# Score tiles from three equally wide matmuls over placed query copies, in a cross-attention kernel

## The chip, the cores and the metric

The kernel runs on one core of a Trainium2 chip. The metric is the device time in microseconds (us). Five engines work side by side: TensorE (PE in the profile, its weight loads PEld), VectorE (DVE), ScalarE (ACT), GpSimd (POOL) and SyncE (SP, which here issues most DMA transfers).

## The reference, cut to what matters

Per batch `b` of 32, 512 positions with 640 channels attend to 77 context positions with 1024 channels, in 20 heads of 32 channels:

```python
q = _heads(hidden_states @ to_q_w)
h_txt = _sdpa(q, _heads(ehs_txt @ to_k_w), _heads(ehs_txt @ to_v_w))
out = _merge(h_txt) @ to_out_w + to_out_b
out = out + residual          # residual = hidden_states
```

`_sdpa` is softmax(q k^T / sqrt(32)) v. The other three context parts of the reference are empty here, since the context has 77 rows, all of them text. All is float32.

## The kernel before, in words

**Parts.** Float32 products are made of two rounded parts: each operand is split into a high part (a rounded copy) and a low part (what the rounding left). A product is the sum of three matmuls: high x high, high x low, low x high. So every query or key needs its high and its low part in SBUF.

**Stages.** A fill computes keys and values of all batches on TensorE, splits them and stores them in DRAM (`k_dram`: 128 channels x high and low x channel chunk x all key rows). Attention then goes batch by batch. A batch has five units, n = 5 b + j, one for each chunk j of 128 channels, that is four heads. For each unit:

- `queries` (L536, token q0 to q4): 15 matmuls of 512 columns into the one `pq` bank of PSUM.
- `high_query` (L777, token Q, ScalarE) writes the high part, `copy_query` (L781, tokens k0, k1, GpSimd) copies halves of it, `low_query` (L785, tokens g0, g1, VectorE) subtracts and writes low parts. Together they fill `qt`, three stationary tiles of 128 rows.
- `score_tile` (L563, tokens s0 to s3, one for each 128 of the 512 positions): three matmuls into one of three `sc` banks: 308 columns (high tile against all four heads' high keys) and twice 154 columns (for two heads each, a tile that holds high queries in one half of its rows and low queries in the other).
- `score_max` (m, VectorE), `exps` (e, ScalarE, one instruction per head with the sum of its row), `sums` (r), `normalize` (N, GpSimd), `block_transpose` (z, VectorE, into the one `z` buffer), and `store_p` (w, four DMA transfers of the probabilities to DRAM).
- Four units later: `load_rows` (d, DMA back, transposed), splitting (c, R on VectorE, l on GpSimd), six value matmuls (v), adding of two halves (A, a), splitting of the result (h, L), and the output projection of a whole batch (p, 120 matmuls of 320 columns), with bias and residual (b, f) and the store (o).
- x of the following batch is loaded (ux), transposed (T) and split (X on ScalarE, x on GpSimd).

**Keys.** The units of a batch form two groups, chunks 0 to 2 and chunks 3 and 4. Each group has one key buffer, `kb0` and `kb1`, of four planes. `load_head_keys` (L514, tokens uk) brings, by one DMA each, one head's high or low keys of the whole group to the rows of its place: eight transfers per group and batch. `copy_half_keys` (L517, token K, GpSimd) then copies 64 rows of two of the planes into planes 0 and 3, so that the wide matmul has only the high keys with zeros around them. All other places stay zero from a memset. The key buffers are single: a group's keys for the next batch are loaded after the last score of the group in this batch.

**What sets the order.** The order of all instructions is written out by hand as three lists of tokens: FILL (batches 0 and 1 among the last products of keys and values), PLAN (the loop, run for batches 2 to 30, 29 times) and LAST_ (batch 31 and the ends). A token names the unit (a digit j, with 5 for the next batch's unit 0) and the step; a query token `jq`, `jQ`, `jk`, `jg` works for the unit after j. Each engine executes its own instructions in the order of the list, and SyncE its transfers. L886 `issue` and L963 `special` translate tokens to calls.

The three matmuls of a score tile before, where `half` is 154 and the keys' planes are the first index of `kb`:

```python
(slice(0, KCOLS), kb[:, 0::3, jg]),
(slice(0, half), kb[:, 1, jg]),
(slice(half, KCOLS), kb[:, 2, jg]),
```

Of the kernel before, what the change touches and what calls it, by code (L numbers as in the profile page):

```python
# [23 lines left out]
P = 128  # L24
Q = 32
# [6 lines left out]
NBLK = HPC * KPAD // Q  # L32

# [18 lines left out]
def kernel(  # L52
# [394 lines left out]
    def open_small():  # L447
        nonlocal small
        if small is None:
            kvc.release()  # L450
            xpool.append(ctx.enter_context(tc.tile_pool(name="xparts", bufs=1, reuse_waits="tile")))
            small = ctx.enter_context(tc.tile_pool(name="small", bufs=1, reuse_waits="tile"))
            kbs.append(small.tile([P, 4, GROUPS[0][1], KCOLS // 2], FPR, name="kb0"))
# [9 lines left out]
    def open_second():  # L463
        nonlocal z
        if not vbs:
# [3 lines left out]
            kbs.append(pool.tile([P, 4, GROUPS[1][1], KCOLS // 2], FPR, name="kb1"))  # L469
# [33 lines left out]
    def load_keys(b, g, heads=range(HPC), parts=(0, 1)):  # L503
        j0, nj = GROUPS[g]
        src = k_dram[g][:, :, :, b * NKEY : (b + 1) * NKEY].bitcast(F32)
        kb = kbs[g].bitcast(F32)
        for i in heads:
            own, half = slice(i * HD, (i + 1) * HD), slice(i % 2 * NKEY, (i % 2 + 1) * NKEY)
            other = slice(*((i + 2) % HPC * HD + k for k in (0, HD)))
            for part, rows in enumerate((own, other)):  # L510
                if part in parts:
                    nc.sync.dma_start(kb[rows, 1 + i // 2, :, half], src[own, part])

    def load_head_keys(b, g, i, part):  # L514
        load_keys(b, g, (i,), (part,))

    def copy_half_keys(g, h):  # L517
        kb, rows = kbs[g], slice(64 * h, 64 * h + 64)
        nc.gpsimd.tensor_copy(kb[rows, 3 * h], kb[rows, 1 + h].bitcast(F32))

    def copy_keys(g):
        copy_half_keys(g, 0)
        copy_half_keys(g, 1)
# [26 lines left out]
    def split_q(n):  # L550

        qt, pq = qts[n % 2], pqs.pop(n)
        nc.scalar.copy(qt[:, 0, :], pq)
        lower, upper = slice(0, 64), slice(64, P)
        halves = ((lower, upper), (upper, lower))
        for w, (r, other) in enumerate(halves):
            nc.gpsimd.tensor_copy(qt[other, 1 + w, :], qt[r, 0, :].bitcast(F32))
        for w, (r, other) in enumerate(halves):
            nc.vector.tensor_tensor(
                qt[r, 1 + w, :], pq[r], qt[r, 0, :].bitcast(F32), ALU.subtract  # L560
            )

    def score_tile(n, t):  # L563
        b, j = divmod(n, NC_)
        g = GROUP_OF[j]
        qt, kb = qts[n % 2], kbs[g]
        jg = j - GROUPS[g][0]
        sc = ps.tile([P, S], F32, tag="sc", name="sc", bufs=3)
        half = KCOLS // 2
        for m, (cols, keys_) in enumerate(  # L570
            (
                (slice(0, KCOLS), kb[:, 0::3, jg]),
                (slice(0, half), kb[:, 1, jg]),
                (slice(half, KCOLS), kb[:, 2, jg]),
            )
        ):
            nc.tensor.matmul(  # L577
                sc[:, cols],
                qt[:, m, t * P : (t + 1) * P],
                keys_,  # L580
                start=(m == 0),
                stop=(m == 2),
            )
        return sc

    def score_max(sc):
        nm = small.tile([P, HPC], F32, tag="nm", name="nm", bufs=3)
        nc.vector.tensor_reduce(  # L588
            nm, sc[:, :KCOLS].rearrange("p (h k) -> p h k", k=NKEY), AX.X, ALU.max, negate=True
        )  # L590
        return nm

    def scores(n, t):
        sc = score_tile(n, t)
        return sc, score_max(sc)

    def exps(n, t, sc, nm):
        if n not in sms:
            sms[n] = small.tile([P, NQ * HPC], F32, tag="sm", name="sm", bufs=2)
        for i in range(HPC):  # L600
            at = t * HPC + i
            nc.scalar.activation(  # L602
                pnb[n % 2][:, at, :NKEY],
                sc[:, i * NKEY : (i + 1) * NKEY],
# [172 lines left out]
    def high_query(n):  # L777
        open_first()
        nc.scalar.copy(qts[n % 2][:, 0, :], pqs[n])  # L779

    def copy_query(n, w):  # L781
        qt, half = qts[n % 2], (slice(0, 64), slice(64, P))
# [345 lines left out]
```

## Time and profile before

| | |
|---|---|
| median of three runs | 1859.1 us (1857.3 to 1859.61) |
| the profiled execution's span | 1856.5 us |
| TensorE busy | 1842.4 us, 10332 matmuls |
| VectorE, ScalarE, GpSimd busy | 1563.4, 1527.2, 1303.9 us |
| TensorE's clock granted | 1.00 |
| DMA | 431.37 MB in 563296 packets |

The span runs from the first instruction's start to the last one's end, and lies 2.6 us under the median of the timed runs. A row of the groups gives the line, engine and operation, the tiles it writes and reads, the shape, the count, the busy time and the mean of one instruction in ns, and after the last bar the idle time of the engine just before, with what ended it. Matmuls are pipelined, so the printed length of one is longer than its distance to the next one; the distance of two starts is what it costs.

### The profile page before, as it was taken

To read this page: it belongs to the slowest core of one execution; us is meant where nothing else is said; L and a number is where in the kernel's file an instruction comes from. 1 tells how busy PE (TensorE), PEld (TensorE's weight loads), DVE (VectorE), ACT (ScalarE), POOL (GpSimd) and SP (SyncE) were. 2 spreads that over 40 slices of the span, in tenths; PEclk is the share of its full clock that TensorE was granted. 3 is DMA by queue.
4 is the path that set the end of the run, shared out by engine and by line. 5 is a ranking of instruction groups with operands and counts; after the bars stand their busy time and mean duration, and the time that the engine had idled before them with its cause. 6 is when DMAs were issued, how large, how long until landed. Compare 5 with 4: busy or idle time off the path is not lost.

```text
span 1856.5 us, 37492 instructions
## 1 busy us (share of the span) xinstructions
PE 1842.4 (99%) x10332; PEld 1655.7 (89%) x10332; DVE 1563.4 (84%) x2502; ACT 1527.2 (82%) x6218; POOL 1303.9 (70%) x1120
## 2 busy tenths in 40 slices
PE   9999999999999999999999999999999999999998
PEld 7888897889999999999999999999999999999998
DVE  5445458899999999999999999999999999999996
ACT  3233248899999999999999999999999999999984
POOL 1100268778788788778778877887778878877874
PEclk9999999999999999999999999999999999999999
DMA  9889779998998898888998888998889988888875
GB/s 188 199 198 249 184 193 256 254 242 235 247 240 243 240 238 232 242 235 236 238 244 237 234 243 237 244 238 237 235 234 244 244 241 236 237 232 243 228 228 187
DMA packets 563296, 431.37 MB, mean 232 GB/s; under 512 B 191120, under 2 KB 471120, under 8 KB 563088
## 3 DMA queue, kind: packets, MB, share of 16 engines
q1 hardware_dynamic: 558192, 413.16, 84.5%
q0 software_dynamic: 4800, 15.65, 2.7%
q8 instruction: 85, 1.39, 0.3%
q14 instruction: 123, 1.01, 0.2%
q10 hardware_dynamic: 96, 0.16, 0.0%
HBM read 247.17 MB, written 181.64 MB: 231 GB/s over the span
## 4 chain that ended last, share of the span: by engine, by line
PE 93%; DMA 4%; SPq 1%; DVE 1%; ACT 1%; issue 0%; POOL 0%; DVEq 0%; ACTq 0%; POOLq 0%
PE po L750 29%; PE pq L542 28%; PE pa L694 12%; PE sc L577 11%; PE pv L204 7%; PE pk L204 6%; DMA pd<-z 1%; DMA cs<-in_ctx_dram 1%; DMA xr<-in_x_dram 1%; DMA wo_s<-wo_dram 0%; DMA wraw<-in_L_xattn_to_v_w_dram 0%; DMA xs<-in_x_dram 0%; DMA wraw<-in_L_xattn_to_k_w_dram 0%; ACT pn L602 0%; DMA raw<-pd 0%
## 5 line engine op out<-in xcount | busy, mean ns | idle before, releaser
L602 ACT ACTIVATE pn<-sc,nm 128x77 f32<-128x77 f32 x2560 | 797.1, 343 | 36.0 <-DVE nm L588 29.6
L750 PE MATMUL po<-wo_s,at 128*128 128x320 f32 x3840 | 707.2, 310 | 0.1
L750 PEld LDWEIGHTS po<-wo_s,at 128*128 128x128 f32 x3840 | 619.7, 188 | 41.1 <-DVE xr L765 0.6
L542 PE MATMUL pq<-xt,wq_s 128*128 128x512 f32 x2400 | 596.7, 394 | 2.9 <-ACT pp L661 1.9
L602 ACT ACTIVATION_READ_ACCUMULATOR pn<-sc,nm 128x1 f32 x2560 | 567.5, 222 | 0.0
L542 PEld LDWEIGHTS pq<-xt,wq_s 128*128 128x128 f32 x2400 | 436.7, 188 | 82.5 <-ACT pp L661 2.1
L617 POOL TENSOR_TENSOR pn<-pn,rs 128x1232 f32<-128x1232 f32 x160 | 389.4, 2434 | 94.0 <-DVE rs L612 90.0
L694 PE MATMUL pa<-pp,vb 128*128 128x512 f32 x960 | 340.9, 403 | 4.1 <-DVE at L731 3.3
L577 PEld LDWEIGHTS sc<-kb,qt 128*128 128x128 f32 x1920 | 302.9, 188 | 14.4 <-ACT pn L602 1.8
L588 DVE TENSOR_REDUCE nm<-sc 128x4 f32<-128x308 f32 x640 | 295.0, 466 | 21.6 <-PE sc L577 16.7
L577 PE MATMUL sc<-kb,qt 128*128 128x154 f32 (+1 forms) x1920 | 301.9, 274 | 0.9 <-ACT pn L602 0.9
L783 POOL CAST qt<-qt 64x512 fp32r<-64x512 f32 x320 | 196.9, 615 | 139.5 <-ACT qt L779 124.4
L712 DVE TENSOR_TENSOR pa<-pa,aw 64x512 f32<-64x512 f32 x320 | 222.3, 695 | 50.4 <-ACT aw L708 43.2
L679 POOL TENSOR_TENSOR pp<-raw,pp 64x512 fp32r<-64x512 f32 x160 | 207.0, 1294 | 66.9 <-ACT pp L661 53.5
L624 DVE STREAM_TRANSPOSE z<-pn 128x1280 f32<-128x1280 f32 x160 | 241.2, 1507 | 8.8 <-DMA pd<-z 3.4
L708 ACT COPY aw<-pa 64x1024 f32<-64x1024 f32 x160 | 162.2, 1014 | 85.0 <-PE pa L694 83.9
L787 DVE TENSOR_TENSOR qt<-pq,qt 64x512 fp32r<-64x512 f32 x320 | 216.8, 678 | 13.9 <-ACT qt L779 9.0
L320 POOL TENSOR_TENSOR xt<-xs,xt 128x512 fp32r<-128x512 f32 x160 | 204.6, 1305 | 20.8 <-ACT xt L316 15.8
L743 POOL TENSOR_TENSOR xr<-xr,bias 128x640 f32<-128x640 f32 x128 | 202.3, 1581 | 13.1 <-issue 3.5
L672 DVE TENSOR_TENSOR pp<-raw,pp 128x1024 fp32r<-128x1024 f32 x160 | 195.7, 1223 | 0.0
L694 PEld LDWEIGHTS pa<-pp,vb 128*128 128x128 f32 x960 | 173.8, 189 | 15.1 <-DVE pp L672 2.3
L663 ACT CAST pp<-raw 128x1024 fp32r<-128x1024 f32 x160 | 168.1, 1051 | 0.7 <-DMA raw<-pd 0.7
(46 smaller groups left out, 1584.2 us busy)
## 6 DMA issues: line engine op xcount, KB each, us to landing
pd<-z SPq DMA_DIRECT2D x640, 160.0 KB, 3.4
raw<-pd SPq DMA_DIRECT2D x160, 512.0 KB, 4.5
xr<-in_x_dram SPq DMA_DIRECT2D x128, 320.0 KB, 3.9
out_dram<-xr SPq DMA_DIRECT2D x127, 320.0 KB, 3.7
xs<-in_x_dram SPq DMA_DIRECT2D x124, 320.0 KB, 5.8
raw<-pd SPq DMA_DIRECT2D x160, 128.0 KB, 4.2
v_dram<-vs SPq DMA_DIRECT2D x80, 192.0 KB, 4.0
k_dram<-ks POOLq DMA_DIRECT2D x20, 512.0 KB, 4.2
```

Source lines behind the costliest of these rows:

```text
L204: nc.tensor.matmul(held[j][:, :gn], w[:, k, a, :], cts[g, k][:, c, :gn], start=(k == 0 and n == 0), stop=(k == NK - 1 and n == 2),)
L542: nc.tensor.matmul(pqs[n], wq_s[:, k, a, j * P : (j + 1) * P], xts[b, k][:, c, :], start=(k == 0 and m == 0), stop=(k == NC_ - 1 and m == 2),)
L577: nc.tensor.matmul(sc[:, cols], qt[:, m, t * P : (t + 1) * P], keys_, start=(m == 0), stop=(m == 2),)
L588: nc.vector.tensor_reduce(nm, sc[:, :KCOLS].rearrange("p (h k) -> p h k", k=NKEY), AX.X, ALU.max, negate=True)
L602: nc.scalar.activation(pnb[n % 2][:, at, :NKEY], sc[:, i * NKEY : (i + 1) * NKEY], AF.Exp, bias=nm[:, i : i + 1], accum_out=sms[n][:, at : ...
L617: nc.gpsimd.tensor_tensor(pf, pf, rs.unsqueeze(2).to_broadcast([P, NQ * HPC, NKEY]), ALU.mult)
L624: nc.vector.transpose(z.rearrange("p b t j -> p t b j"), pn.rearrange("p (t h) k -> p t (h k)", t=NQ).rearrange("p t (b i) -> p t b i", i=Q),)
L679: nc.gpsimd.tensor_tensor(pp[64:, 4, :], raw[:64, 2, :], pp[:64, 4, :].bitcast(F32), ALU.subtract)
L694: nc.tensor.matmul(pas[n][:, p, :], vb[:, p, t, :], pp[:, c, :], start=(c == p), stop=(c == p + 2),)
L712: nc.vector.tensor_tensor(pa[64 * p : 64 * p + 64, 0], pa[:64, p], aw[:, p], ALU.add)
L750: nc.tensor.matmul(pos[b, t, h][:, :HALF], ats[b * NC_ + j][:, a, t * P : (t + 1) * P], wos[0][:, j, c, h * HALF : (h + 1) * HALF], start= ...
L787: nc.vector.tensor_tensor(qt[rows, 1 + w, :], pqs[n][rows], qt[rows, 0, :].bitcast(F32), ALU.subtract)
```

## The change

Of the twelve head blocks that a score tile needs (four heads x high-high, high-low, low-high), each of the three matmuls now takes four, one in each 32 rows of its stationary tile. The heads' scores stand in the bank in the order 2, 0, 1, 3, in blocks of 78 columns (77 keys and one zero). Matmul 0 writes blocks 0 to 2 (234 columns), matmul 1 blocks 1 to 3 (234), matmul 2 blocks 0 and 3 (156).

Tile 0 holds the high queries, but in rows 96 to 128 the low part of head 1. Tile 1 is a copy of the high tile, with the low part of head 0 in rows 64 to 96. Tile 2 has the high parts of heads 2 and 3 in rows 0 to 64, their low parts in rows 64 to 128. They are made in two ways: three copies and two low parts (g0 writes low parts of all rows into tile 2, k2 copies 32 rows of these to tile 1), or two copies and three low parts (g3, g2). The copy of the whole tile (k0) can also be done by ScalarE from PSUM (the new token B). In every case g1 overwrites rows 96 to 128 of tile 0 after the copies have read them.

Keys come in ten transfers per group instead of eight. Two of them (the pairs) bring high and low keys of a head at once, to the regions of matmul 0 and matmul 1. The key copies (K) are gone. Twelve blocks of 32 rows are read from DRAM per group, instead of eight.

The list PLAN is drawn anew, all engines' orders in it. In PLAN the units have, for query tokens: unit 0 `g0 k0 k2 k1 g1`, unit 1 `B g0 k2 k1 g1`, unit 2 `k0 g0 k2 k1 g1`, unit 3 `g3 k0 g2 k1 g1`, unit 4 `g0 k0 k2 k1 g1`. FILL and LAST_ keep their order; in them `g0` and `g1` became `g3` and the four tokens `k1 k0 g2 g1` at (nearly everywhere) one place, the key tokens have new numbers, and K is taken out.

```diff
+KBLK = NKEY + 1
+ORDER = (2, 0, 1, 3)
+WIDTHS = (3 * KBLK, 3 * KBLK, 2 * KBLK)
+KEYS_OF = (
+    (0, None, 0, 0, 1),
...
+COPIES = ((1, 0, 0, 0, P), (2, 0, 0, 64, 64), (1, 64, 2, 0, Q))
+LOWS = ((2, 0, 0, P), (0, 96, 32, Q), (1, 64, 0, Q), (2, 64, 64, 64))
+def keys_at(nj, m):
+    return (0, nj * WIDTHS[0] + KBLK, 2 * nj * WIDTHS[0] + KBLK)[m]
...
+    def load_head_keys(b, g, piece):
+        nj = GROUPS[g][1]
+        i, part, quad, m, block = KEYS_OF[piece]
+        src = k_dram[g][i * HD : (i + 1) * HD].rearrange("p a j n -> p (a j) n")
+        n0, nn = (0, 2 * nj) if part is None else (part * nj, nj)
+        c0, w = keys_at(nj, m) + block * KBLK, WIDTHS[m]
+        dst = kbs[g].bitcast(F32)[quad * HD : (quad + 1) * HD]
+        nc.sync.dma_start(
+            dst[:, c0 : c0 + nn * w].rearrange("p (r k) -> p r k", k=w)[:, :, :NKEY],
+            src[:, n0 : n0 + nn, b * NKEY : (b + 1) * NKEY].bitcast(F32),
+        )
...
-        for m, (cols, keys_) in enumerate(
-            (
-                (slice(0, KCOLS), kb[:, 0::3, jg]),
-                (slice(0, half), kb[:, 1, jg]),
-                (slice(half, KCOLS), kb[:, 2, jg]),
-            )
-        ):
+        for m, heads in enumerate((blocks[:, 0:3], blocks[:, 1:4], blocks[:, 0::3])):
+            c0 = keys_at(nj, m) + (j - j0) * WIDTHS[m]
             nc.tensor.matmul(
-                sc[:, cols],
+                heads,
                 qt[:, m, t * P : (t + 1) * P],
-                keys_,
+                kb[:, c0 : c0 + WIDTHS[m]].rearrange("p (h k) -> p h k", k=KBLK),
                 start=(m == 0),
                 stop=(m == 2),
+                skip_group_check=True,
             )
...
-    def high_query(n):
+    def high_query(n, m=0):
         open_first()
-        nc.scalar.copy(qts[n % 2][:, 0, :], pqs[n])
+        nc.scalar.copy(qts[n % 2][:, m, :], pqs[n])
 
     def copy_query(n, w):
-        qt, half = qts[n % 2], (slice(0, 64), slice(64, P))
-        nc.gpsimd.tensor_copy(qt[half[1 - w], 1 + w, :], qt[half[w], 0, :].bitcast(F32))
+        qt, (m1, r1, m0, r0, rn) = qts[n % 2], COPIES[w]
+        nc.gpsimd.tensor_copy(qt[r1 : r1 + rn, m1, :], qt[r0 : r0 + rn, m0, :].bitcast(F32))
 
     def low_query(n, w):
-        qt, rows = qts[n % 2], slice(64 * w, 64 * w + 64)
-        nc.vector.tensor_tensor(qt[rows, 1 + w, :], pqs[n][rows], qt[rows, 0, :].bitcast(F32), ALU.subtract)
+        qt, (m1, r1, r0, rn) = qts[n % 2], LOWS[w]
+        rows = slice(r0, r0 + rn)
+        nc.vector.tensor_tensor(
+            qt[r1 : r1 + rn, m1, :], pqs[n][rows], qt[rows, 0, :].bitcast(F32), ALU.subtract
+        )
```

The end of the loop in the new PLAN, to which the prediction refers:

```
"4k0 3w2 4v3 4f00 4d1 4f01 4m3 4e2 4v4 4v5 3uk08 3w0 4k2 4s1 4A 4k1 4g1 4ux1 4p10 4p11 4p12 4p13 4e3 "
"3uk09 4p15 5c1 5c0 4m1 5q0 5q1 3w3 3uk06 3uk04 5q2 4ux2 5q3 4a0 3uk03 4o0 3uk07 4N 4a1 5d1 5h 5d0 "
"5uk17 4z 4e1 5R 5q4 4w1 4b1 4w2 4w0 5L 5s0 5l 4w3 5uk19 4ux0 5s1 5m0 5Q 4p14 "
```

And the start of LAST_ in the new kernel:

```
"a0r a1d0 a0v1 a0e0 a0m1 a0v0 a0N a0uk11 a0g3 a0v2 a0v3 a0v5 a0uk18 a0v4 a0k1 a0k0 a0g2 a0g1 a0p16 "
"a0ur3 a0A a0s2 a1uv13 a0f10 a0p17 a0m2 a1uv16 a1c0 a0p18 a0z a0e2 a1q0 a1l a1q1 a0a1 a0e1 a0w0 a0s3 "
```

More of the change, by code (lines that the diff above doesn't have):

```diff
@@ L501, in open_late @@
             wos.append(late[0].tile([P, NC_, 2, C], FPR, name="wo_s"))
[L503 to L523, printed above, removed]
+    def load_head_keys(b, g, piece):
[9 more added lines that the diff above has]
+        )
     def load_values(b, g, segments=SEGMENTS):
@@ L548, in queries, with score_blocks @@
                 )
[L550 to L560, printed above, removed]
-            )
+    def score_blocks(sc):
+        return sc[:, : HPC * KBLK].rearrange("p (h k) -> p h k", k=KBLK)
     def score_tile(n, t):
@@ L587, in score_max @@
         nm = small.tile([P, HPC], F32, tag="nm", name="nm", bufs=3)
[L588 to L595 removed]
+        nc.vector.tensor_reduce(nm, score_blocks(sc)[:, :, :NKEY], AX.X, ALU.max, negate=True)
+        return nm
     def exps(n, t, sc, nm):
```

33 lines of the change are left out of this document (23 added, 10 removed), and 161 rows, old and new, of tables (FILL, LAST_, PLAN).

## The prediction

> **What bounds the kernel now.** I read the page first, then the time of each engine by stretches, then the order of TensorE's work, its queue of weight loads, and last SyncE's queue.
>
> ```profile
> span 1856.5 us, 37492 instructions
> PE 1842.4 (99%) x10332; PEld 1655.7 (89%) x10332; DVE 1563.4 (84%) x2502; ACT 1527.2 (82%) x6218; POOL 1303.9 (70%) x1120
> PE 93%; DMA 4%; SPq 1%; DVE 1%; ACT 1%; issue 0%; POOL 0%; DVEq 0%; ACTq 0%; POOLq 0%
> ```
>
> The chain that ended last is TensorE for 93% of the span. Busy matmuls can hide waits, so I look at stretches: the second batch of the fill, one turn of the repeated loop, and the first 49 us of the last batch.
>
> ```profile
> 301.00:351.00 50.00, 44.86 (x232) 37.23 (x231) 43.63 (x68) 45.53 (x191) 41.54 (x38) 1.00 0.93 262
> 1087.00:1136.00 49.00, 49.00 (x287) 44.61 (x286) 44.90 (x73) 45.32 (x191) 39.31 (x33) 1.00 0.86 235
> 1773.00:1822.00 49.00, 49.00 (x300) 45.44 (x299) 43.35 (x72) 43.79 (x187) 34.68 (x27) 1.00 0.76 222
> ```
>
> After the times of PE, weight loads, DVE, ACT and POOL come the granted clock (1.00 throughout) and the DMA share. In the loop TensorE never rests, while VectorE is free for 4.1 us of 49, ScalarE for 3.7, GpSimd for 9.7. So a batch lasts as long as its matmuls, and the question is what one matmul costs from its start to the next one's.
>
> ```profile
> 1016.49 2.93 PE L542 MATMUL pq<-xt,wq_s 128*128 128x512 f32 x12
> 1019.25 0.48 PE L577 MATMUL sc<-kb,qt 128*128 128x308 f32 x3
> ...
> 1020.98 0.60 PE L750 MATMUL po<-wo_s,at 128*128 128x320 f32 x3
> 1021.42 0.39 PE L694 MATMUL pa<-pp,vb 128*128 128x512 f32 x1
> 1021.65 0.60 PE L750 MATMUL po<-wo_s,at 128*128 128x320 f32 x3
> ...
> 1087.38 0.86 PE L577 MATMUL sc<-kb,qt 128*128 128x308 f32 x6
> 1088.08 0.65 PE L750 MATMUL po<-wo_s,at 128*128 128x320 f32 x3
> 1088.56 0.49 PE L577 MATMUL sc<-kb,qt 128*128 128x308 f32 x3
> ```
>
> Starts count here, since the printed lengths overlap. 512 columns: (1019.25 - 1016.49)/12 = 0.230 us. 320 columns: 0.44/3 = 0.147 us. So a column costs 0.083/192 = 0.43 ns, and 9 ns come on top per matmul. Two score tiles, six matmuls, took 0.70 us until the next kind, and the three output matmuls behind them took 0.48 instead of 0.44: their start was recorded 0.04 us before they ran. One score tile thus costs (0.70 + 0.04)/2 = 0.37 us. Check from the counts of a whole run:
>
> ```profile
> L750 PE MATMUL po<-wo_s,at 128*128 128x320 f32 x3840 | 707.2, 310 | 0.1
> L542 PE MATMUL pq<-xt,wq_s 128*128 128x512 f32 x2400 | 596.7, 394 | 2.9 <-ACT pp L661 1.9
> L694 PE MATMUL pa<-pp,vb 128*128 128x512 f32 x960 | 340.9, 403 | 4.1 <-DVE at L731 3.3
> L577 PE MATMUL sc<-kb,qt 128*128 128x154 f32 (+1 forms) x1920 | 301.9, 274 | 0.9 <-ACT pn L602 0.9
> ```
>
> Over 32 batches these are 120, 75, 30 and 60 matmuls a batch: 49.0 - 120 x 0.147 - 75 x 0.229 - 30 x 0.230 = 7.3 us, over 20 tiles 0.365 us. I take 0.367.
>
> **Why a tile costs that, and what it costs after.** By columns alone, 308 + 154 + 154 = 616 would be 616 x 0.43 + 3 x 9 = 292 ns. The missing 75 ns are in the weight loads:
>
> ```profile
> 1001.72 0.19 PEld L694 LDWEIGHTS pa<-pp,vb 128*128 128x128 f32 x1
> 1001.83 0.57 PEld L750 LDWEIGHTS po<-wo_s,at 128*128 128x128 f32 x3
> ...
> 1002.98 0.19 PEld L694 LDWEIGHTS pa<-pp,vb 128*128 128x128 f32 x1
> 1003.09 0.58 PEld L750 LDWEIGHTS po<-wo_s,at 128*128 128x128 f32 x3
> ```
>
> Behind a score tile, loads follow each other at 0.11 us. A 154-column matmul streams in 75 ns but must wait for a load of 110: 141 + 2 x 113 = 367. The 308-column matmul has time to spare that the short ones cannot use. The change levels this: 234 columns stream in 234 x 0.43 + 9 = 110 ns, just a load's time, and 156 wait for their load, 110. Three times 0.110 to 0.113 is 0.330 to 0.340; I take 0.335, a gain of 0.032 us a tile. The bounds are 0.040 (columns and loads overlap perfectly, 0.327) and 0.022 (three matmuls at 0.115). No row has a 234-column matmul; 154 and 308 on either side obey the same two prices.
>
> [...]
>
> **Loop.** 20 tiles x 0.032 = 0.64 us a batch; the loop runs 29 batches: -18.6 us. Last batch: 20 x 0.032 = -0.6. Fill: TensorE has waits there (44.86 of 50), so half of two batches, -0.6.
>
> **What the other engines get.**
>
> ```profile
> L617 POOL TENSOR_TENSOR pn<-pn,rs 128x1232 f32<-128x1232 f32 x160 | 389.4, 2434 | 94.0 <-DVE rs L612 90.0
> L783 POOL CAST qt<-qt 64x512 fp32r<-64x512 f32 x320 | 196.9, 615 | 139.5 <-ACT qt L779 124.4
> L624 DVE STREAM_TRANSPOSE z<-pn 128x1280 f32<-128x1280 f32 x160 | 241.2, 1507 | 8.8 <-DMA pd<-z 3.4
> L787 DVE TENSOR_TENSOR qt<-pq,qt 64x512 fp32r<-64x512 f32 x320 | 216.8, 678 | 13.9 <-ACT qt L779 9.0
> L320 POOL TENSOR_TENSOR xt<-xs,xt 128x512 fp32r<-128x512 f32 x160 | 204.6, 1305 | 20.8 <-ACT xt L316 15.8
> L519 POOL CAST kb<-kb 64x462 fp32r<-64x462 f32 x64 | 36.8, 576 | 4.9 <-DMA kb<-k_dram 1.2
> L519 POOL CAST kb<-kb 64x308 fp32r<-64x308 f32 x64 | 28.3, 443 | 6.7 <-DMA kb<-k_dram 3.1
> L779 ACT CAST qt<-pq 128x512 fp32r<-128x512 f32 x160 | 95.3, 596 | 6.9 <-PE pq L542 6.4
> ```
>
> Per loop: 13 query copies on GpSimd for 10 (+3 x 0.615) and no key copies (-2 x 0.576 - 2 x 0.443): -0.2 us. VectorE: 11 low parts for 10, +0.68, so 45.6 busy. ScalarE: one more high part (token B), +0.60, so 45.9. I take a copy or a low part at the same price for 32, 64 or 128 rows: at 512 columns the 64-row and the 128-row GpSimd subtractions of the loop are both near 1.3 us (1305 above). All remain under the 48.36 us that TensorE would need.
>
> **Order and waits.** A new wait appears: g1 writes low parts over rows 96 to 128 of the high tile and must follow the copies that read them, so Q, g, k and the last g make one chain, about 0.60 + 2 x 0.62 + 2 x 0.68 = 3.2 us at worst where 2.0 sufficed. Behind g1 on VectorE wait score maxima and the normalized tile's transpose; for g1 wait the next scores and the next q0, since pq has one bank. I walked the new loop with these durations, placing TensorE's instructions back to back. Unit 3: q4 ends at 29.8 us of the loop; Q 30.5; GpSimd, coming from low x part 2x1 at 31.4, k0 and k1 until 32.6; g1 33.3; 4q0 is due at 34.15. The other four: g1 at 2.6 against q0 at 3.8; 13.3 against 2s0 at 13.9; 23.9 against 24.9; 41.8 against 43.8. Margins of 0.6 to 2.0 us: no stall, so the loop costs nothing beyond its matmuls. If that cover failed by 0.5 us once a batch it would be 14.5 us, three quarters of the gain.
>
> The last batch is not redrawn but edited: there k1, k0, g2 and g1 stand behind N, GpSimd's normalization.
>
> ```profile
> 1774.94 2.28 POOL L617 TENSOR_TENSOR pn<-pn,rs 128x1232 f32<-128x1232 f32 x1 [0.52 <-DVE rs L612]
> ...
> 1777.28 0.61 POOL L783 CAST qt<-qt 64x512 fp32r<-64x512 f32 x1
> ...
> 1777.55 0.63 PE L542 MATMUL pq<-xt,wq_s 128*128 128x512 f32 x2
> ```
>
> This is unit 0 of the last batch: N ends at 1777.22, two copies end at 1778.5, g1 at 1779.25; q0 ran at 1777.55 and would now wait 1.7 us. Unit 1 has the same order (N, two copies, g1: 4.3 us, against 2.9 us of matmuls): 1.5. Units 2 and 3 have 3.4 to 4.5 us of matmuls in between and wait for nothing. Last batch: +3.2, bounds 0 and 5. The fill has two or three such places (b0, b1, b2), with waits there already: +2, bounds 0 and 5.
>
> **Transfers.** 20 key loads for 16 a batch. Twelve head blocks of 32 rows are read instead of eight: 4 x 32 x 5 = 640 more packets.
>
> ```profile
> q1 hardware_dynamic: 558192, 413.16, 84.5%
> L512 SPq DMA_DIRECT2D kb<-k_dram x409: 302/447/2686, 402.8 to 1648.2; - x137
> DMA to landing us min/median/max: 1.8/3.1/6.6
> ...
> 1282.17 1.10 SPq L302 DMA_DIRECT2D xs<-in_x_dram  x2
> 1283.36 0.57 SPq L512 DMA_DIRECT2D kb<-k_dram  x1
> DMA to landing us min/median/max: 6.0/6.0/6.0
> ```
>
> A mean packet costs 0.845 x 16 x 1856.5/558192 = 45 ns of one engine, so 640 are at most 1.8 us a batch and the DMA share goes from 0.86 to about 0.90. On SyncE four more issues of 0.45 to 0.5 us fit. The median load lands in 3.1 us, but the one right behind two x loads took 6.0. In the new order the last piece of group 0 (3uk07) stands close behind such a load, and 14 issues after the first store of unit 3's probabilities: those can go when z is transposed (33.3 + 1.5 = 34.8), so 34.8 + 14 x 0.5 = 41.8. The next batch's first score is due at 47.3, 5.5 us later. With 3 to 5 us it is in time: cost 0, bounds 0 and (6.6 - 5.5) = 1.1 us a batch.
>
> **Sum.** -18.6 - 0.6 - 0.6 + 3.2 + 2 = -14.6 us: span 1841.9. The profiled execution's span lies 2.6 us under the median of the timed runs, 1859.1; with the same 2.6, 1844.5 us.
>
> **Rivals.** *A, keys late (slower).* The same loop, but 3uk07 lands 6 to 6.6 us after its issue, at 47.8 to 48.4, and every batch's first score waits. It decides from 5.5 us of landing; at 6.5 it is 29 x 1.0 = 29 us: 1873. For it: the row with 6.0, the DMA share near 0.9. Against it: two issues stand between the x load and this piece, and the median is 3.1. Chance 0.13.
> *B, the chain eats the gain.* The maxima and g1 meet on VectorE at 94% busy and a tight place (2s0, 0.6 us of margin) slips 0.4 us a batch: 29 x 0.4 = 12 us: 1856, about no change. For it: margins below one instruction. Against it: TensorE now waits nowhere with the same engines at 92%. Chance 0.12.
> *C, columns rule.* A 234-column matmul is not relieved by the levelling: 8 x 0.43 ns x 640 = +2 us, and the ends' +5: 1866. Against it: 0.367 for 616 columns. Chance 0.03.
> *D, the ends cost nothing and the tile gains 0.040:* 31 x 20 x 0.040 = 25 us: 1834. Chance 0.05.
>
> **Numbers.** The forecast, 1844.5, has 0.67; its own range is 1837 to 1853 (tile gain 0.022 to 0.040, ends 0 to 10). About 0.2%, 3.7 us, is what a measurement of this kernel can tell from no change. Faster: the forecast, D, and a third of B, 0.75; same: most of B, 0.09; slower: A and C, 0.16. The range 1836 to 1860 leaves out A, C and D.
>
> **What would show it.** Right: the score matmuls at about 0.335 us a tile by their starts, a batch every 48.4 us, PE busy throughout the loop, waits of 1 to 2 us of pq matmuls for qt's low parts in the last batch. Wrong: pq or sc waiting for qt or kb in every batch; a batch over 48.8 us; a tile still at 0.36.

## The result, and the profile after

The changed kernel takes 1929.8 us, median of four runs (1927.88 to 1932.98), against 1858.7 before: the ratio is 1.0384, with a 95% interval of 1.0369 to 1.0399. It is 71 us slower, where the prediction said 14.6 us faster. The page of the profiled execution begins:

```profile
span 1926.1 us, 37390 instructions
PE 1856.9 (96%) x10332; PEld 1644.6 (85%) x10332; DVE 1614.8 (84%) x2546; ACT 1547.8 (80%) x6247; POOL 1395.8 (72%) x1079
PE 30%; DVE 25%; DMA 12%; POOL 10%; ACT 9%; SPq 7%; issue 7%; POOLq 0%; DVEq 0%; ACTq 0%
```

TensorE was 93% of the chain that ended last; now it is 30%, and VectorE and GpSimd have 35% between them. GpSimd is busy 92 us longer (1395.8 against 1303.9) with 41 instructions fewer. That is the line to stop at: fewer instructions in more time.

To place the 69.6 us of span, I took the starts of the score matmuls from the trace. There are 60 in a batch, so every 60th starts a new batch. The start of batch 0 divides off the keys and values. "Fill" is from there to batch 3's first score, "loop" the 28 turns from there to batch 31's, "rest" what follows.

| us | before | after | difference |
|---|---|---|---|
| to batch 0 | 256.2 | 256.3 | +0.1 |
| fill | 145.1 | 167.9 | +22.8 |
| loop, 28 turns | 1372.0 (49.0 each) | 1408.6 (50.3) | +36.6 |
| rest | 83.2 | 93.2 | +10.0 |

The score tile itself did become cheaper. The timeline of TensorE in a stretch of the loop without waits (start, length, line, shapes, count):

```profile
1065.48 0.46 PE L577 MATMUL sc<-kb,qt 128*128 128x234 f32 x3
1065.78 0.89 PE L557 MATMUL pq<-xt,wq_s 128*128 128x512 f32 x3
1066.51 0.46 PE L577 MATMUL sc<-kb,qt 128*128 128x234 f32 x3
```

By starts the three score matmuls take 0.30 us, and the three query matmuls behind them 0.73 instead of 3 x 0.230 = 0.69: 0.04 belongs to the tile, which makes 0.34 us. It was 0.367, and 0.335 was forecast. So the loss lies in waits. TensorE's waits of the whole run (what it waited for: us in total, times, longest):

```profile
PE pa L689 <- DVE at L726: 24.8, 32, 1.3
PE pq L557 <- DVE qt L783: 19.4, 8, 4.3
PE sc L577 <- DVE qt L783: 9.9, 29, 0.7
```

Counts tell the place. 29 and 32 are about once in each batch: 0.34 us before the first score of unit 2 and 0.78 before the first value matmul of the next batch's unit 0. The 8 waits of 19.4 us are in the fill (6 of them, 13.6 us) and the last batch (2, 5.8 us). Before, all of TensorE's waits for `qt` were one of 0.9 us. The idle times printed for the two places are too short, since the ends of matmuls are modelled. By starts, against a run below that has the same order and matmuls and no such waits, the first place costs 0.54 us a turn, the second 1.05, and three smaller ones 0.2: together the whole 1.8 us that a turn lasts beyond its matmuls.

### The profile page after: what moved, and what is told of

It is laid out like the page before. It is cut to its first block, busy times and chain, and to the rows that moved or that the text cites. A ratio compares the mean times of both kernels' runs of the same rounds, so it can differ in the third digit from the quotient of the medians.

```text
span 1926.1 us, 37390 instructions
## 1 busy us (share of the span) xinstructions
PE 1856.9 (96%) x10332; PEld 1644.6 (85%) x10332; DVE 1614.8 (84%) x2546; ACT 1547.8 (80%) x6247; POOL 1395.8 (72%) x1079
## 4 chain that ended last, share of the span: by engine, by line
PE 30%; DVE 25%; DMA 12%; POOL 10%; ACT 9%; SPq 7%; issue 7%; POOLq 0%; DVEq 0%; ACTq 0%
PE pk L229 7%; PE pq L557 6%; PE pv L229 6%; PE po L745 6%; DVE z L619 6%; DVE pa L707 5%; POOL qt L778 5%; ACT pn L597 4%; POOL pn L612 4%; DVE qt L783 4%; PE pa L689 3%; DVE nm L589 3%; DVE pp L667 3%; SPq L628 3%; DMA out_dram<-xr 2%
## 5 line engine op out<-in xcount | busy, mean ns | idle before, releaser
L745 PE MATMUL po<-wo_s,at 128*128 128x320 f32 x3840 | 672.3, 311 | 0.1
L557 PE MATMUL pq<-xt,wq_s 128*128 128x512 f32 x2400 | 639.2, 400 | 19.5 <-DVE qt L783 19.4
L597 ACT ACTIVATION_READ_ACCUMULATOR pn<-sc,nm 128x1 f32 x2560 | 596.6, 235 | 0.0
L612 POOL TENSOR_TENSOR pn<-pn,rs 128x1232 f32<-128x1232 f32 x160 | 365.2, 2283 | 112.1 <-DVE rs L607 104.7
L778 POOL CAST qt<-qt 64x512 fp32r<-64x512 f32 (+2 forms) x407 | 323.5, 795 | 136.4 <-ACT qt L774 90.1
L689 PE MATMUL pa<-pp,vb 128*128 128x512 f32 x960 | 300.1, 405 | 30.8 <-DVE at L726 24.8
L783 DVE TENSOR_TENSOR qt<-pq,qt 32x512 fp32r<-32x512 f32 (+2 forms) x364 | 247.6, 680 | 86.3 <-POOL qt L778 53.0
L577 PE MATMUL sc<-kb,qt 128*128 128x234 f32 (+1 forms) x1920 | 286.6, 266 | 12.2 <-DVE qt L783 9.9
L674 POOL TENSOR_TENSOR pp<-raw,pp 64x512 fp32r<-64x512 f32 x160 | 239.5, 1497 | 35.7 <-ACT pp L656 18.5
L345 POOL TENSOR_TENSOR xt<-xs,xt 128x512 fp32r<-128x512 f32 x160 | 229.9, 1454 | 25.3 <-ACT xt L341 19.2
L667 DVE TENSOR_TENSOR pp<-raw,pp 128x1024 fp32r<-128x1024 f32 x160 | 223.3, 1396 | 4.2
```

The source lines that it names most:

```text
L557: nc.tensor.matmul(pqs[n], wq_s[:, k, a, j * P : (j + 1) * P], xts[b, k][:, c, :], start=(k == 0 and m == 0), stop=(k == NC_ - 1 and m == 2),)
L577: nc.tensor.matmul(heads, qt[:, m, t * P : (t + 1) * P], kb[:, c0 : c0 + WIDTHS[m]].rearrange("p (h k) -> p h k", k=KBLK), start=(m == 0), ...
L597: nc.scalar.activation(pnb[n % 2][:, at, :NKEY], sc[:, i * KBLK : i * KBLK + NKEY], AF.Exp, bias=nm[:, i : i + 1], accum_out=sms[n][:, at ...
L612: nc.gpsimd.tensor_tensor(pf, pf, rs.unsqueeze(2).to_broadcast([P, NQ * HPC, NKEY]), ALU.mult)
L667: nc.vector.tensor_tensor(pp[:, 2:4, :], raw[:, 0:2, :], pp[:, 0:2, :].bitcast(F32), ALU.subtract)
L689: nc.tensor.matmul(pas[n][:, p, :], vb[:, p, t, :], pp[:, c, :], start=(c == p), stop=(c == p + 2),)
```

## What GpSimd and VectorE do to each other

The groups of GpSimd by shape, and behind them one group of VectorE (busy us, mean ns of one):

```profile
L674 POOL TENSOR_TENSOR pp<-raw,pp 64x512 fp32r<-64x512 f32 x160 | 239.5, 1497 | 35.7 <-ACT pp L656 18.5 <-issue 5.2
L778 POOL CAST qt<-qt 32x512 fp32r<-32x512 f32 x116 | 119.4, 1029 | 31.0 <-DVE qt L783 28.9
L778 POOL CAST qt<-qt 128x512 fp32r<-128x512 f32 x131 | 104.6, 798 | 81.3 <-ACT qt L774 75.8
L778 POOL CAST qt<-qt 64x512 fp32r<-64x512 f32 x160 | 99.5, 622 | 24.1 <-ACT qt L774 14.2
```

```profile
L667 DVE TENSOR_TENSOR pp<-raw,pp 128x1024 fp32r<-128x1024 f32 x160 | 223.3, 1396 | 4.2
```

The 32-row copy takes longest, 1029 ns, and the 64-row one 622: rows are not what costs. L667 is R, the subtraction that makes the low parts of the probabilities, with both inputs in SBUF. In the kernel before it is L672:

```profile
L672 DVE TENSOR_TENSOR pp<-raw,pp 128x1024 fp32r<-128x1024 f32 x160 | 195.7, 1223 | 0.0
```

Single instructions show what happens. The timelines of VectorE and of GpSimd at one R of unit 2:

```profile
1040.15 1.22 DVE L667 TENSOR_TENSOR pp<-raw,pp 128x1024 fp32r<-128x1024 f32 x1
...
1042.54 0.69 DVE L783 TENSOR_TENSOR qt<-pq,qt 32x512 fp32r<-32x512 f32 x1 [0.78 <-POOL qt L778]
```

```profile
1040.40 2.11 POOL L778 CAST qt<-qt 32x512 fp32r<-32x512 f32 x2 [0.31 <-DVE qt L783]
```

```profile
1043.37 0.87 PE L577 MATMUL sc<-kb,qt 128*128 128x234 f32 x6 [0.31 <-DVE qt L783]
```

The copy k2 begins at 1040.40, while R runs, and the two copies last 2.11 us where two undisturbed ones last 1.28. The first of them ends at 1041.84, 0.47 us after R. Then g1 waits 0.78 us for the copies, and the next score tile waits for g1. Over the trace behind the first 400 us: of 377 query copies the 86 that touch an R in time have a median of 1461 ns, the other 291 have 611. A busy VectorE alone does not do it: 257 of these 291 ran for more than 0.3 us beside some other instruction of VectorE. It goes the other way as well: in the loop, an R that begins while GpSimd computes takes up to 1.74 us, and 1.21 alone. Whichever comes second is longer by most of what is left of the first: in the loop 83 of these copies had 0.97 to 1.02 us of R left and took 0.83 to 0.87 us longer, and 58 R had 0.48 to 0.66 us of l left and took 0.36 to 0.53 us longer. The recorded starts do not always tell which that is: in the kernel with the new widths alone, below, 28 copies that begin 0.5 us ahead of an R last 2.18 us and end 0.48 us behind it, while that R takes its 1.21; why is open. In the kernel before, 28 of 146 normalizations N began beside an R, with 3.06 us against 2.28, once a turn and off the path; of 288 copies one was prolonged.

In what follows, the exclusion means this: where R and a GpSimd instruction met, one of them took longer, a copy 1461 ns for 611 in the median, R up to 1.74 us for 1.21. By what means, no run shows.

My theory for the loop: the new order puts k2, a low part of x and l beside R; their extra time runs around a cycle through VectorE and GpSimd (g0, k2, k1, g1, z, R), and this cycle, not TensorE, sets the turn. The rivals: the number of copies and low parts sets it; the late copy k0 of unit 4 alone does; the wider matmuls are dearer than they look (rival C of the prediction).

## Experiments

Spans are those of the profiled executions. Where no interval is given, the time is one run.

| kernel | span | fill | turn, mean of 28 | rest |
|---|---|---|---|---|
| before | 1856.5 | 145.1 | 49.00 | 83.2 |
| after | 1926.1 | 167.9 | 50.31 | 93.2 |
| before, new widths alone | 1857.7 | 144.6 | 48.93 | 86.1 |
| after, old widths | 1932.3 | 173.3 | 50.33 | 94.0 |
| after without k2 | 1903.4 | 166.5 | 49.47 | 94.3 |
| after, unit 4's tile 1 by ScalarE | 1925.9 | 169.1 | 50.23 | 92.7 |
| after, R with one input | 1878.3 | 161.8 | 48.72 | 92.7 |
| new widths alone, R with one input | 1840.5 | 144.4 | 48.47 | 81.6 |
| after, copies first at the ends | 1919.1 | 165.4 | 50.40 | 86.4 |
| after, order redrawn | 2134.2 | 173.3 | 57.53 | 93.2 |
| the same, ScalarE at the ends | 2134.6 | 168.6 | 57.84 | 89.0 |
| after, three engines' order redrawn | 1922.2 | 167.5 | 50.06 | 95.2 |
| the same, ScalarE at the ends | 1902.6 | 160.6 | 49.94 | 86.4 |
| R with one input, ScalarE at the ends | 1862.8 | 157.9 | 48.66 | 84.9 |

**The widths without the rest of the change.** The kernel before, with its own copies, keys and order, and only the three matmuls cut differently. The keys do not stand where these blocks would want them, so the scores are not the reference's.

```diff
...
-                (slice(0, KCOLS), kb[:, 0::3, jg]),
-                (slice(0, half), kb[:, 1, jg]),
-                (slice(half, KCOLS), kb[:, 2, jg]),
...
+        blocks = sc[:, : HPC * 78].rearrange("p (h k) -> p h k", k=78)
...
+            keys_ = (kb[:, 0:3, jg, 0:78], kb[:, 1:4, jg, 0:78], kb[:, 0::3, jg, 0:78])[m]
...
```

> The kernel before, with its own order, copies, key loads and key copies, but each score tile made of three matmuls of 234, 234 and 156 columns (its scores are not those of the reference). Theory, the short matmuls waited for weight loads: every loop turn falls from 49.0 to 48.4 to 48.5 us, the span from 1856.5 to about 1839. Rival, columns alone count: 49.0 to 49.1 a turn, span 1857 to 1859.

Measured: 1859.49 us, against 1860.46 for the kernel before on the same chip. The turn is 48.93 us, not 48.4. TensorE's first wait in the list:

```profile
PE sc L572 <- POOL qt L779: 5.5, 29, 0.2
```

Once a turn, 29 times, the scores wait for a query copy (one of the 28 of 2.18 us beside R), which the cheaper tiles have made the next thing late. By starts that place is 0.45 us longer than its matmuls, so the bare matmuls of a turn are 48.5. Rival C is out, and so is the thought that the widths alone would bring what the tile saves.

**The old widths in the new kernel.** 308, 154 and 154 columns with the new copies, transfers and order; again the scores are not the reference's.

```diff
...
-        for m, heads in enumerate((blocks[:, 0:3], blocks[:, 1:4], blocks[:, 0::3])):
-            c0 = keys_at(nj, m) + (j - j0) * WIDTHS[m]
+        for m, (cols, c0, w) in enumerate(
+            ((slice(0, 2 * half), 0, 2 * half), (slice(0, half), 0, half), (slice(half, 2 * half), half, half))
+        ):
+            c0 += keys_at(nj, m) + (j - j0) * WIDTHS[m] - (0, 0, half)[m]
...
```

> The changed kernel with everything that is new, but its score tiles made of 308, 154 and 154 columns again (so its scores are not those of the reference); TensorE then has 0.56 us more work a turn. Theory, a chain through VectorE, GpSimd and ScalarE sets the turn and not TensorE: 50.3 to 50.5 us as in the changed kernel. Rival, TensorE's own time plus waits of a fixed length: 50.9.

Measured: 1934.07 us, turn 50.33, as with the new widths. Twenty tiles that cost 0.027 us more each change nothing in the loop. TensorE does not set the turn.

**Without the copy k2.** All k2 are taken out of PLAN; 32 rows of tile 1 then hold old values.

```diff
-        "0r 0v0 0v1 1uv10 0uk12 1uv16 0g0 0m1 0v2 0s2 0m2 0v3 0f10 0ux3 0v4 1uv15 0k0 0p16 0e0 1uv14 0k2 "
+        "0r 0v0 0v1 1uv10 0uk12 1uv16 0g0 0m1 0v2 0s2 0m2 0v3 0f10 0ux3 0v4 1uv15 0k0 0p16 0e0 1uv14 1uv12 "
...
```

> The changed kernel without the 32-row copies k2 in the loop (low part of head 0 is left out of tile 1 there). Theory, the query chain on GpSimd with its collisions: the wait of 0.47 us before unit 2's first score goes, the wait of about 1.0 us before the next batch's first value matmul shrinks to about 0.4; a turn of 49.0 to 49.4 instead of 50.3. Rival, VectorE's work as a whole sets the turn: it does not change, 50.2 to 50.3.

Measured: 1905.23 us, turn 49.47. Four copies less gain 0.84 us a turn. The waits of the scores for `qt` are gone and the 24.8 us before the value matmuls have become 12.4. The meetings with R do not go with k2: 86 copies still begin beside one, as in the kernel after. 57 of them are now 64-row copies, whose mean rises from 622 to 934 ns. The chain of each of these units is one copy shorter, while what is left of it still meets R. So the run fits both the exclusion and the mere number of copies: it does not tell these apart.

**Unit 4's copy of the whole tile by ScalarE.** I had traced the 0.78 us before the value matmuls back to k0 of unit 4, which lasts 1.46 us beside an R.

```diff
-        "... 4c1 4v0 4Q 4R 2uv05 4l ... 4k0 3w2 4v3 ..."
+        "... 4c1 4v0 4Q 4B 4R 2uv05 4l ... 3w2 4v3 ..."
```

> The changed kernel with the whole-tile copy of unit 4 (4k0, 1.46 us on GpSimd in the changed kernel's trace where it overlaps VectorE's R, 0.61 elsewhere) made by ScalarE from PSUM instead (token 4B right behind 4Q). Theory, this copy delays k2, k1, N, z, R and L of unit 4: the wait before the next first value matmul falls from 1.0 us to 0 to 0.3, a turn of 49.3 to 49.6. Rival, VectorE or ScalarE is full: ScalarE's 0.6 us more is lost again, 50.1 to 50.6.

Measured: 1927.92 us, turn 50.23; the wait before the value matmuls is as long as before (24.4 us, 32 times). This part of the theory fell. k2 waits for g0 and not for k0, and g0 stands behind R on VectorE. A prolonged instruction costs only where something waits for it in the end.

**R with one input.** This separates the exclusion from the number of copies: all copies, low parts and the order stay, and R keeps its place and length on VectorE, but becomes a stream transpose of the high parts into a spare tile. The low parts of the probabilities in chunks 0 and 1 of `pp` are left out, and the value matmuls read the high parts instead.

```diff
...
-        nc.vector.tensor_tensor(
-            pp[:, 2:4, :], raw[:, 0:2, :], pp[:, 0:2, :].bitcast(F32), ALU.subtract
+        spare = vals[0].tile([P, 2, S], F32, tag="spare", name="spare", bufs=1)
+        nc.vector.transpose(
+            spare.rearrange("p k q -> p (k q)"),
+            pp[:, 0:2, :].rearrange("p k q -> p (k q)").bitcast(F32),
...
-            pp[:, c, :],
+            pp[:, 2 if c == 4 else c % 2, :],
...
```

> The changed kernel, but VectorE's R, a subtraction with both inputs in SBUF, is a stream transpose with one input in SBUF and about the same length, 1.2 us (the low parts of the probabilities are left out; the value matmuls that used them read the high parts). Theory, R and a GpSimd instruction exclude each other: copies, low x parts and last_p that lie beside R return to 0.61, 1.30 and 1.29 us (now 1.46, 2.13, 2.39), and the turn falls from 50.3 to 48.5 to 48.9 us. Rival, the chain through VectorE and GpSimd is too long by its own work: 50.1 to 50.3.

Measured: 1880.33 us, turn 48.72. The same groups as above in this kernel, GpSimd first, then VectorE, then the engines' busy time in one turn:

```profile
L676 POOL TENSOR_TENSOR pp<-raw,pp 64x512 fp32r<-64x512 f32 x160 | 206.5, 1291 | 36.5 <-ACT pp L656 10.7 <-issue 6.8 <-DMA pd<-z 3.9
...
L780 POOL CAST qt<-qt 64x512 fp32r<-64x512 f32 x160 | 97.7, 611 | 24.1 <-ACT qt L776 14.2
L780 POOL CAST qt<-qt 128x512 fp32r<-128x512 f32 x131 | 80.1, 612 | 141.9 <-ACT qt L776 140.3
L780 POOL CAST qt<-qt 32x512 fp32r<-32x512 f32 x116 | 70.4, 607 | 47.3 <-DVE qt L785 45.6
```

```profile
L668 DVE STREAM_TRANSPOSE spare<-pp 128x1024 f32<-128x1024 f32 x160 | 196.0, 1225 | 6.1 <-ACT pp L658 4.5
```

```profile
1000.00:1048.50 48.50, 48.50 (x287) 43.98 (x286) 45.33 (x74) 46.03 (x192) 38.23 (x33) 1.00 0.92 247
```

Every copy is back at 0.61 us, whether it has 32, 64 or 128 rows; the stand-in for R takes 1225 ns, as R did before; and TensorE is busy for the whole 48.5 us. Not one copy is prolonged, though 142 now begin beside the stand-in. Between the two kernels stands what R is: a subtraction of two SBUF inputs or a transpose of one. Whether the number of inputs is what counts in it is not shown: no run changes that number alone. Two more things differ: the value matmuls no longer wait for R, but in the kernel after such waits were 4.0 us in the whole run; and R no longer reads `raw`, for whose loads TensorE's waits there were 0.6 us. So the exclusion of R and GpSimd is shown as the cause of the loop's loss: 28 x (50.31 - 48.72) = 44.5 us. Eight of the 28 turns are longer than 48.5, up to 50.9. Most of them have a wait of this row, longer by starts than it is printed:

```profile
PE sc L577 <- DMA kb<-k_dram: 2.6, 5, 1.0
```

That is rival A of the prediction, keys late, five times in the run instead of every batch.

**Both in the kernel before.** The new widths alone, and R with one input.

> The kernel before with the three new widths alone (turn 48.9, with one wait of 0.45 us a turn for a query copy), and R with one input as in the run above. Theory, the same exclusion makes that wait: 48.4 to 48.5 a turn, TensorE's bare matmuls. Rival, the old order's copies are late by themselves: 48.9.

Measured: 1842.3 us against 1858.73 before, turn 48.47, and no wait in the loop. The tile's gain is real: (49.00 - 48.47)/20 = 0.027 us. The exclusion hid it even without the new copies: with the widths alone the turn was 48.93.

**Copies first at the ends.** In FILL and LAST_, k1 and k0 go right behind Q, and N behind them where it stood ahead.

```diff
...
-        "b0m1 b0e0 b0r YL4 b0s2 b0N b2T3 ... b0Q b0v2 b0m2 YD41 "
-        "b0v5 b0v4 b0g3 b0s3 YD40 b0A b0k1 b0k0 b0g2 b0g1 ..."
+        "b0m1 b0e0 b0r YL4 b0s2 b2T3 ... b0Q b0k1 b0k0 b0N b0v2 "
+        "b0m2 YD41 b0v5 b0v4 b0g3 b0s3 YD40 b0A b0g2 b0g1 ..."
...
```

> The changed kernel with the loop as it is; in the fill and the last batch k1 and k0 stand right behind Q and, where the normalization N stood before them, ahead of N. Theory, at the ends q0 waits for g1 because the copies queue behind N and x parts on GpSimd: of the 22.9 us that the fill lost up to the third batch's first score some 10 to 15 come back, of the last batch's 10.0 some 3 to 6; span 1926 to 1905 to 1913. Rival, the low parts and copies themselves are too much for the ends: 1922 to 1926.

Measured: 1921.9 us. The rest fell from 93.2 to 86.4, as expected; the fill only from 167.9 to 165.4, a miss. Why, the trace of the kernel after shows at the longest wait of its fill, on TensorE, GpSimd and VectorE:

```profile
317.66 4.18 PE L557 MATMUL pq<-xt,wq_s 128*128 128x512 f32 x9 [4.27 <-DVE qt L783]
```

```profile
311.00 2.49 POOL L612 TENSOR_TENSOR pn<-pn,rs 128x1232 f32<-128x1232 f32 x1 [1.24 <-DVE rs L607]
313.45 1.31 POOL L296 DMA_DIRECT2D v_dram<-vs  x2
314.81 1.28 POOL L778 CAST qt<-qt 64x512 fp32r<-64x512 f32 x2
```

```profile
313.96 0.69 DVE L783 TENSOR_TENSOR qt<-pq,qt 64x512 fp32r<-64x512 f32 x1
316.12 1.40 DVE L783 TENSOR_TENSOR qt<-pq,qt 32x512 fp32r<-32x512 f32 x2 [1.46 <-POOL qt L778]
```

The high part is written by 313.53, the first low part by 314.65. N ends at 313.49, before the high part is there. Then two stores of values, which GpSimd issues (1.31 us), and two copies (1.28) go by until g2 and g1 may overwrite what the copies have read, and only when these end, at 317.52, is the one `pq` bank free. At the same place of the list in the kernel before (TensorE, VectorE, GpSimd):

```profile
308.50 2.31 PE L542 MATMUL pq<-xt,wq_s 128*128 128x512 f32 x9 [0.94 <-DVE qt L787]
```

```profile
306.96 1.39 DVE L787 TENSOR_TENSOR qt<-pq,qt 64x512 fp32r<-64x512 f32 x2
```

```profile
308.43 0.61 POOL L783 CAST qt<-qt 64x512 fp32r<-64x512 f32 x1
```

There both low parts follow the high part at once, and the bank was free before the copies had begun. In the old scheme the copies were not on the way from one query product to the next; in the new one they are. An earlier place in the list does not take them off it: with the copies first, nothing stands between the high part and the copies at this place, and the wait, still the longest of its kind, is 3.0 us:

```profile
PE pq L557 <- DVE qt L783: 8.8, 5, 3.0
```

**The order redrawn.** All operations stay, and PLAN is drawn anew so that as few copies as possible begin during an R; TensorE's order and the transfers were moved too.

```diff
-        "0r 0v0 0v1 1uv10 0uk12 1uv16 0g0 0m1 0v2 0s2 0m2 0v3 0f10 0ux3 0v4 1uv15 0k0 0p16 0e0 1uv14 0k2 "
+        "0m1 0e0 0v0 0uk14 0g0 1uv11 0v1 0v2 0s2 0r 0ux3 0v3 0v4 0f10 0p16 0v5 0s3 0e1 0A 0p17 1c0 0p18 0p19 "
...
```

> The kernel after with the same operations, all of them, in the loop, but its hand-written order redrawn so that as few GpSimd copies and low parts as possible begin while the running maximum's rest product R (both inputs in SBUF) is on VectorE, and no such pair lies on the cycle through VectorE and GpSimd. If the exclusion between R and GpSimd sets the turn, the turn falls from 50.3 us to 48.5 to 48.9 us and the span by 28 x 1.4 to 1.8 = 39 to 50 us, to 1876 to 1887 us, with fill and ends as in the kernel after. If the copies were slow for another reason, or the number of copies set the turn, a new order alone leaves it at 50.0 to 50.3 us.

> As the run before it, and in the fill and the last batch ScalarE writes query tile 1 right behind the high tile where it stands in the tables, with the one GpSimd copy behind it, so that the chain from a query product to its last low part has one GpSimd copy in it instead of two (about 0.6 us less for each of 14 units, and no GpSimd copy behind another one's normalization). Fill up to the third batch 150 to 162 us (after 167.9, before 145.1), last batch and ends 84 to 88 us (after 93.2), turn as in the run before it: span 1855 to 1873 us. If the fill's gaps are set by something else than this chain, the fill stays at 165 to 168 us.

Measured: 2132.9 us, ratio 1.146 (1.143 to 1.149), and 2128.6, ratio 1.142 (1.139 to 1.146). Both missed widely, the second in its fill as well, where the third batch already runs in the new order. SyncE's queue, first in the kernel after, then here:

```profile
SPq L643 <- DMA pd<-z: 10.6, 7, 4.4
```

```profile
SPq L643 <- DMA pd<-z: 144.9, 62, 3.9
```

SyncE stood waiting to load probabilities whose store was still under way, with x, keys and values queued behind. What cost TensorE most in this run were waits for values, 63.4 us in 45 waits. Between 1000 and 1060 us:

```profile
PE pa L689 <- DMA vb<-v_dram: 2.3, 2, 1.8
```

That SyncE's waits alone made the turn longer is not shown; in the kernel before, the same line waited 46.5 us, 65 times, without a loss. These two runs say nothing of the exclusion.

**The order of three engines alone.** TensorE's and SyncE's orders are those of the kernel after; only VectorE, ScalarE and GpSimd instructions change places. In the expectation R is called the running maximum's rest product; it is the low part of the probabilities.

```diff
-        "1p31 2k2 2k1 2uv04 2p32 2v0 2R 2v1 2p37 2d1 1w0 1w2 1w3 2e2 2p38 2d0 2v2 0uk16 0uk15 2m1 2e3 2v3 2T3 "
+        "2c1 2q2 2q3 2e0 1a0 2q4 2m3 2m2 2r 2s1 1p30 1a1 2h 0uk11 2p35 1b3 2uv00 2p36 2Q 2R 2e3 1w1 1p31 "
+        "2uv04 2L 2p32 2v0 2m1 1T1 2N 2g0 2v1 2e2 2p37 1T2 2d1 1w0 1w2 1w3 2p38 2k0 2d0 2k2 2v2 2e1 2k1 0uk16 "
...
```

> In the redrawn order before, TensorE's order and SP's transfers were moved as well, and the turn became 57.4 us with the SP queue waiting on transfers; that run said nothing of the exclusion. Here TensorE's and SP's orders are those of the kernel after, token by token, and only instructions of VectorE, ScalarE and GpSimd change places among their own (R sooner or later, the second key half's low part l before a normalization N, and the like), so that no collision of R with GpSimd lies on the cycle. By the exclusion: turn 48.5 to 49.0 us, span 1926.1 - 28 x 1.3 to 1.8 = 1876 to 1890 us. If the number of copies or of low parts sets the turn, 50.0 to 50.3 us and 1918 to 1926. If SP's queue has no slack for any new order, over 50.3.

> The loop of the run beside it, and in the fill and the last batch ScalarE writes query tile 1 behind the high tile, as in the earlier run with mended ends. Fill up to the third batch 158 to 165 us (after 167.9), last batch and ends 84 to 88 us (after 93.2), turn as in the run beside it: span 1858 to 1880 us.

For the second, `B` stands behind `Q` for `k0` in FILL and LAST_ (all but the first unit of LAST_):

```diff
-        "... a0s0 a0Q Yn1 ... YC02 a0g3 a0k1 a0s2 Ys33 a0k0 a0g2 a0g1 ..."
+        "... a0s0 a0Q a0B a0k1 Yn1 ... YC02 a0g3 a0s2 Ys33 a0g2 a0g1 ..."
```

Measured: 1918.9 us, ratio 1.031 (1.030 to 1.033), turn 50.06, a miss; and 1903.2, ratio 1.024 (1.022 to 1.026). The first kernel's groups:

```profile
L612 POOL TENSOR_TENSOR pn<-pn,rs 128x1232 f32<-128x1232 f32 x160 | 394.4, 2465 | 51.7 <-DVE rs L607 44.6
...
L778 POOL CAST qt<-qt 128x512 fp32r<-128x512 f32 x131 | 89.7, 685 | 22.3 <-ACT qt L774 17.7
L778 POOL CAST qt<-qt 32x512 fp32r<-32x512 f32 x116 | 77.8, 670 | 44.9 <-POOL pn L612 18.0 <-issue 11.9 <-DVE qt L783 11.1
```

The copies meet R less often (670 and 685 ns, from 1029 and 798), but now N meets it (2465, from 2283). GpSimd is busy for 1311.6 us instead of 1395.8, and yet the turn fell by only 0.25 in the mean, 0.5 in the median (49.78). An order that moves the collisions is thus worth little; what sets these 50.06 us is not settled. At the ends ScalarE's copy helped as expected, fill 160.6 and rest 86.4, though the span, with this turn, missed. TensorE's wait from above is then

```profile
316.87 3.62 PE L557 MATMUL pq<-xt,wq_s 128*128 128x512 f32 x9 [2.90 <-DVE qt L783]
```

2.90 us for 4.27.

**Both causes taken away.** R with one input (with the same part left out) and ScalarE at the ends.

> Both causes taken away in one kernel: R reads one input (a stream transpose into a spare tile; the low parts of the text probabilities are left out and the value matmuls read the high parts, so the output is not the reference's), and in the fill and the last batch ScalarE writes query tile 1. If the loss of the change is the exclusion of R and GpSimd in the loop plus the chain of copies and low parts at the ends, and the two add: turn 48.4 to 48.6 us, fill up to the third batch 152 to 157 us (161.8 with R alone, and 6 to 7 less for tile 1), last batch and ends 84 to 88 us, span 1851 to 1861 us. If they are one cause, the ends gain nothing over the run with R alone: 1878 us.

Measured: rest 84.9, as expected; turn 48.5 in most batches and 48.66 in the mean, fill 157.9 and span 1862.8, each a little above its bounds and far from the second case. The timed runs have a median of 1869.1, ratio 1.006 (1.004 to 1.008). So the two causes nearly add: apart, they took 47.8 us (R) and 19.6 (ScalarE at the ends, in the pair above), together 63.3, of the 69.6 that were lost. These are spans of single executions; by the medians of the timed runs ScalarE at the ends brought 15.7 and both together 60.7, of 71.1. What is left against the kernel before is 6.3 us of span. The fill is still 12.8 us longer, with one copy and three low parts between two query products, and the loop 9.5 shorter; that was not taken apart further.

No kernel that computes the whole reference beat the kernel before. The best with the change's score tiles is 1903.2. The run of 1842.3 leaves out low parts of the probabilities and has neither the placed copies nor the placed keys: it shows what the tile alone is worth where R does not hold GpSimd up. With the whole change and R with one input the span is 1862.8, still above the 1856.5 before.

## Why the prediction was wrong, point by point

- *What bounds the kernel before, and the tile.* Right. The tile fell from 0.367 to 0.340, gain 0.027, inside the bounds 0.022 to 0.040. The loop at its bare matmuls lasts 48.5, not 48.36: about 3 us in all.
- *Copies and low parts at the same price for any rows.* Right for the copies when undisturbed: 607, 611 and 612 ns for 32, 64 and 128 rows; low parts take 685, 695 and 667.
- *The walk through the new loop* is the step that failed: "Margins of 0.6 to 2.0 us: no stall, so the loop costs nothing beyond its matmuls." It gave GpSimd's instructions their mean length wherever they stood, without asking what VectorE does beside them. A copy beside R lasts 1.46 us instead of 0.61, and the margin at 2s0 was 0.6. The walk also ended with the turn; the larger wait, 0.78 us as printed and 1.05 by starts, stands in the next turn's first value matmul, which it never reached. Predicted -18.6 us over 29 turns, measured +36.6 over 28.
- *Rival B* named the right place, 2s0, and nearly the size of that wait, 0.34 as printed and 0.54 by starts for 0.4. That is luck: B's cause was VectorE's load and its price 0.4 us a batch. What came is a cycle that the whole turn has to wait for, 50.31 us against 48.47 of bare matmuls: 1.84 us a batch, over four times B's price.
- *Last batch, +3.2, bounds 0 and 5.* The right mechanism, sized too small: the rest grew by 10.0, and putting the copies ahead of N took 6.8 of it away. The walk let one low part follow the two copies, where two do, g2 and g1. The waits before the next q0 were 2.42 and 3.38 us instead of 1.7 and 1.5, and TensorE's clock was at 0.50 for 3.4 us behind the second.
- *Fill, +2, bounds 0 and 5.* Measured +22.8. The prediction counted three units, those whose copies stand behind N. But in all ten the copies and two low parts came between two query products, where the bank had waited for two low parts alone. And a wait in the fill cost more than itself: 20.4 us of the fill ran at half clock, as the last section shows, none before.
- *Transfers, 0.* Right: in the kernel after, keys ended two waits, 0.5 us in all, and the DMA share of a turn is 0.90 as forecast, with 704 more packets a batch for the 640 counted. Only with the turn at 48.5 did keys end waits of up to 1.0 us, five times.
- *Rivals C and D* are out: C by the tile's 0.340 us and the bare turn of 48.5, D by the ends and by a tile gain of 0.027.

## What to carry to other kernels

Before a copy or a subtraction is given to GpSimd, look at which VectorE instructions run beside it and whether one of them prolongs it (here R did, 1461 ns for 611, and none of those beside 257 other copies), and price it beside such a one at its own time plus what is left of that (here the copies and the R of the loop took 0.13 us less than that, and the 28 copies with the new widths alone 0.36 more); a mean from a trace in which the two happened not to meet is no price. When a step gets a new reader or writer that must come first, follow the buffer it holds (here the one bank of `pq`) to the next product, in every place of the order and past the end of the turn. And where a change joins a cheaper operation with dearer preparations, run the cheaper operation by itself: here it would have shown at once that the next thing late was a query copy.

## What was not expected of the hardware

The cost of TensorE's waits does not end with them. Behind the 4.27 us without a matmul, nine matmuls of 512 columns took 3.98 us to the next kind (317.66 to 321.64), 0.44 each instead of 0.230. The stretches view of these four microseconds, with the granted clock as third number from the end:

```profile
318.00:322.00 4.00, 4.00 (x11) 3.17 (x11) 2.83 (x4) 2.34 (x10) 2.52 (x2) 0.50 0.55 186
```

In the kernel before it was 1.00 for as long as matmuls ran, through a wait of 1.94 us (up to 318.43) too. Here it is 0.50 from 315.7 to 322.5, and again in the fill for 6.8, 3.4 and 3.4 us from 329.4, 343.0 and 387.4 on, each time at or behind a wait; at 315.7 TensorE had rested 2.3 us. In the loop, whose longest wait is printed as 0.8 us, it stayed at 1.00.

The loop of the kernel with the order redrawn has a clock below 1.00 too, with no wait over 1.8 us in this turn:

```profile
1000.00:1057.00 57.00, 50.45 (x271) 44.03 (x271) 43.52 (x70) 44.28 (x182) 37.03 (x31) 0.94 0.76 199
```

Between 400 and 2040 us of that run the clock was at 0.50 in 23 stretches, 99 us in all; the mean over its span is 0.971, against 0.994 in the kernel after. So part of its long turns is the clock. How much rest lowers the clock is not shown: in the kernel after the clock fell behind a wait of 1.83 us (up to 342.20), and in the kernel before it did not behind one of 1.94.
